# Row counts on the GpSimd queue in the last two layers of a four-layer graph network, and a few steps moved behind the output attention's preparation

## The chip, the cores and the metric

The kernel runs as one launch on one core of one Trainium2 chip. The metric is the device time of one execution in microseconds (us). A core has TensorE (PE: matmul, with weight loads shown as PEld), VectorE (DVE), ScalarE (ACT), GpSimd (POOL) and SyncE (SP). SP and POOL also issue transfers here: each has its own queue of DMA issues, taken in order.

## The reference, cut to what matters

Four graph layers over N = 4096 nodes with D = 64 features, all with the same adjacency matrix `adj` (4096 x 4096 float32, zeros and ones). Each layer is `x = x + layer(relu(layernorm(x)), adj)`.

```python
# layer 0: eight attention heads of 32 features, then an output attention
e = leaky_relu(f1[:, None] + f2[None, :], 0.2)        # per head
h = concat(elu(softmax(where(adj > 0, e, -9e15)) @ Wh) for the 8 heads)
Who = h @ W_out
e_o = leaky_relu((Who @ a1)[:, None] + (Who @ a2)[None, :], 0.2)
out0 = tanh(softmax(where(adj > 0, e_o, -9e15)) @ Who)
# layer 1: hyperbolic attention (logmap, sigmoid scores * adj, expmap), radius r, w_att, b_att
# layer 2: mean over neighbours
deg = clip(adj.sum(1) + 1, 1)
out2 = l2_normalise(relu(concat([X, (adj @ X + X) / deg]) @ W + b))
# layer 3: decaying sum over the last 100 neighbours of each row
rank = cumsum(adj != 0, axis=1); deg = rank[:, -1:]; k = minimum(deg, 100)
w = mask * where(rank - (deg - k) > 0, 0.5 ** (deg - rank), 0)
out3 = w @ (X @ weight) + bias
```

## The kernel before, in words

The nodes are held as `NB = 32` blocks of `P = 128`. Source nodes lie on the partitions, target nodes along the free axis, in groups of `G = 512` columns (`GB = 4` blocks). The kernel stores a byte mask of the edges, `mask_d`, in device memory early on; the later stages load it as tiles of `JT = 4` source blocks, so `NQ = 8` tiles make one pass over all sources.

**Counting odd entries.** The fast path assumes that `adj` holds only zeros and ones. `count_odd` (L946) proves it: it loads one block of 128 rows by `HW = 2048` columns of the float32 matrix (1 MB, tile `raw`, two buffers) and one VectorE instruction (L950) counts the entries that differ from their own `> 0`, into one column of `bad`. There are 64 such rows, taken one after the other from the iterator `todo`; every stage that has room takes some. At the end `bad` is reduced, and if anything was counted a general kernel runs instead. Before, 16 rows are counted in the output attention (every second mask tile), 11 in layer 2 and 37 in layer 3. All rows are loaded from SP's queue, the mask tiles too.

**Order.** The kernel is traced in a tile framework, and a scheduler decides at build time in what order each engine takes its instructions, buffers permitting. `behind(mark)` and `tc.issue_after(mark)` keep the instructions in their block behind a marked one, on the mark's own engine. `in_order()` keeps the traced order on PE, DVE and ACT inside its block. `staggered(...)` interleaves generators.

**Layer 0.** Each head is finished by a step (around L1711) that transposes the finished features `num` into a tile `hT` (`by_g[:, 3]`) with PE and multiplies it by `W_out`. Then comes the output attention's preparation (L1919 to L2011): a maximum over all partitions (`omax`, made by a GpSimd all-reduce, whose result L1932's neighbours wait for), the factors `YB`, `YC`, `YD1`, `YD2`, the sum over all nodes `wsum` (L1985) with its mean `meano`, and last `YCn` (L2006), whose instruction is called `prepared`. Ahead of it, in the traced order, stand the constants of layer 1 (L1746 to L1768: the radius `rt` and eleven values derived from it, loads of `wab` and `bt`) and the clearing of the tile `MOV` (L1777, 128 x 4096 bf16, on GpSimd).

The output attention has four units `u` of `HO2 = 1024` target columns. For each of the eight mask tiles `mo` (512 KB, three buffers) a unit inverts the mask into `nmo8`, stores it as `noedge_d` from POOL's queue, makes the attention's bit patterns `st` (ACT, L1200), `B` (DVE, L1206) and `C` (DVE, L1214), and lets PE accumulate `accB`, `accC` (L2097) and `dd` (L2110, L2116). `meano` is used only at the unit's end, by one product that is added to `accC`. The unit is then evicted (`evD`, `evB`, `evC`), and `finish_unit` and the node work of layer 1 run beside the next unit.

**Layer 1** works on pairs of node blocks with PE, DVE and ACT and uses the tiles `XAf`, `LDf` and `MOV`.

**Layer 2** (L2617 to L2668) has two halves of 2048 target columns: PE multiplies the mask tiles `m2` (1 MB) with the features (`nacc`, L2628) and counts degrees with a selector `sel` (`dc`, L2641). Each half is then evicted and goes through `layer2_group` four times: a serial chain of mean, concatenation `cat`, product, relu, norm, residual and layer norm, which ends with layer 3's support, in two parts `SS` and `lo` (L2609 ff.).

**Layer 3** (L2671 to L2741) has four units of 1024 columns. For each mask tile `m3` (512 KB, three buffers) and each of its four blocks `j`, PE makes the rank from the end (`pv`, L2697 and L2705), ACT turns it into the weight `w3b` (L2714), and PE accumulates `sacc` (L2679). A unit is evicted into `ev3` (L2724), folded by PE (`pn`, L2729), given bias and residual by DVE (`og`, L2737 and L2738), and stored in two pieces of 128 KB from POOL's queue (L2739). Row counts in layers 2 and 3 are held behind the last layer-norm or support instruction that is ready (`not_before_nodes`, `valued[-1]`).

Of the kernel before, what the change touches and what calls it, by code (L numbers as in the profile page):

```python
# [9 lines left out]
F32 = mybir.dt.float32  # L10
BF16 = mybir.dt.bfloat16
F16 = mybir.dt.float16
# [6 lines left out]
ALU = mybir.AluOpType  # L19
# [5 lines left out]
P = 128  # L25
N = 4096
NB = N // P
D = 64
# [10 lines left out]
PROJ_EPS = 0.004  # L39
# [12 lines left out]
HW = N // 2  # L52
# [778 lines left out]
def kernel(  # L831
# [24 lines left out]
    nc = tc.nc  # L856
    NH, F, O = W_sp.shape[0] + W_int.shape[0], W_sp.shape[1], W_sp.shape[2]
# [85 lines left out]

        return col.unsqueeze(2).to_broadcast([P, col.shape[1], width])

    def count_odd(pool, c):  # L946

        raw = pool.tile([P, HW], F32, name="raw", tag="raw", bufs=2)
        nc.sync.dma_start(raw, adjT[c % NB * P : (c % NB + 1) * P, c // NB * HW : (c // NB + 1) * HW])
        nc.vector.scalar_tensor_tensor(  # L950
            raw, raw, 0.0, raw, ALU.is_gt, ALU.not_equal, accum_out=bad[:, c : c + 1]
        )

    todo = iter(range(2 * NB))
# [81 lines left out]
    with ExitStack() as l0:  # L1036
        lp = l0.enter_context(tc.tile_pool(name="l0", bufs=1))
# [402 lines left out]
        with ExitStack() as ha:  # L1440
# [34 lines left out]
            for hf in range(2):  # L1475
# [9 lines left out]
                for hd in range(NH):  # L1485
# [61 lines left out]
                    for j0 in range(0, NB, 2):  # L1547
                        q = j0 // JT
# [111 lines left out]
                    def finish_unit(hf=hf, hd=hd, ev=ev, fme=fme):  # L1660
# [50 lines left out]
                            return  # L1711
                        c = hd // 4
                        for bq in range(NS):
                            hT = by_g[:, 3]
                            transpose_to(
                                hT, [num[:, bq * GB + b, :] for b in range(GB)], P, ps, nc.scalar.copy
                            )
                            pw = ps.tile([P, GB, D + 2], F32, name="pwho", tag="misc")
                            for b in range(GB):
                                nc.tensor.matmul(  # L1720
                                    pw[:, b, :],
                                    lhsT=hT[:, b * P : (b + 1) * P],
                                    rhs=rho[:, c, :],
                                    start=True,
                                    stop=True,
                                )
# [13 lines left out]
        lq = ctx.enter_context(tc.tile_pool(name="l1", bufs=1))  # L1740
        KA = D + 2

        def scalar_tile(name):
            return lq.tile([P, 1], F32, name=name)

        rt, rabs, sqc, cc = (scalar_tile(n) for n in ("rt", "rabs", "sqc", "cc"))  # L1746
        nc.gpsimd.dma_start(rt, r_in.unsqueeze(0).to_broadcast([P, 1]))
        nc.vector.scalar_tensor_tensor(rabs, rt, -1.0, rt, ALU.mult, ALU.max)
        nc.vector.reciprocal(sqc, rabs)
        nc.vector.tensor_tensor(cc, rt, rt, ALU.mult)  # L1750
        nc.vector.reciprocal(cc, cc)
        c2, m2c, p2c, m4c, cneg, maxn, hrow = (
            scalar_tile(n) for n in ("c2", "m2c", "p2c", "m4c", "cneg", "maxn", "hrow")
        )
        nc.vector.tensor_tensor(c2, cc, cc, ALU.mult)
        nc.vector.tensor_scalar(m2c, cc, -2.0, None, ALU.mult)
        nc.vector.tensor_scalar(m4c, cc, -4.0, None, ALU.mult)
        nc.vector.tensor_scalar(p2c, cc, 2.0, None, ALU.mult)
        nc.vector.tensor_scalar(cneg, cc, -1.0, None, ALU.mult)
        nc.vector.tensor_scalar(maxn, rabs, 1.0 - PROJ_EPS, None, ALU.mult)  # L1760
        nc.vector.tensor_scalar(hrow, rabs, 0.5, None, ALU.mult)
        wab = lq.tile([P, 2, D], F32, name="wab")
        nc.gpsimd.dma_start(
            wab.rearrange("p s d -> p (s d)"),
            w_att.rearrange("k o -> (k o)").unsqueeze(0).to_broadcast([P, 2 * D]),
        )
        bt = scalar_tile("bt")
        nc.gpsimd.dma_start(bt, b_att.unsqueeze(0).to_broadcast([P, 1]))  # L1768
# [8 lines left out]
        nc.gpsimd.memset(MOV, 0.0)  # L1777

        def layer1_nodes(bs, work, augs):

# [93 lines left out]
        with ExitStack() as ob:  # L1874
# [47 lines left out]
            with in_order():  # L1922
# [58 lines left out]
                )  # L1981
                nc.scalar.activation(wno, wno, AF.Exp, scale=1.0 - ALPHA)

                wsum = spool.tile([P, D], F32, name="wsum")
                nc.vector.tensor_reduce(wsum, vals.rearrange("p b d -> p d b"), AX.X, ALU.add)  # L1985
                pss = ps.tile([P, D], F32, name="psso", tag="misc")
# [18 lines left out]
            YCn = hp.tile([P, NB // 8, 2, 2 * D], F16, name="YCn")  # L2005
            prepared = nc.vector.tensor_scalar(  # L2006
                YCn,
                YC.rearrange("p (n i) s d -> p n i (s d)", i=2)[:, 1::4],
                -1.0,
                None,  # L2010
                ALU.mult,  # L2011
            )

            def finish_unit(u, evs):

# [44 lines left out]
            for u in range(4):  # L2060
# [6 lines left out]

                dd = ps_acc.tile([P, G], F32, name="ddo", tag="acc")
                for q in range(NQ):
                    if q % 2 == 0:  # L2070
                        with behind(prepared.ins):
                            count_odd(work, next(todo))
                    m = work.tile([P, JT, HO2], U8, name="mo", tag="mo", bufs=3)
# [48 lines left out]
                    if q == 0 and pending:  # L2122
                        finish_unit(*pending)
                        beside = layer1_nodes(slice((u - 1) * OB, u * OB), work, augs)
                        pending = None
                    elif u:
                        for _ in range(2):
                            next(beside, None)
# [332 lines left out]
    def layers_fast(es, wide, *sums):  # L2461
# [23 lines left out]
        nc.gpsimd.dma_start(w3, W3)  # L2485
        b3t = lp.tile([P, D], F32, name="b3f")
        nc.gpsimd.dma_start(b3t, b3.unsqueeze(0).to_broadcast([P, D]))
        sel = lp.tile([P, NB * O], BF16, name="sel")
        nc.gpsimd.memset(sel, 0.0)
        nc.gpsimd.memset(sel[:, :: O + 1], 1.0)  # L2490

# [76 lines left out]
        def layer2_group(b0, part, deg):  # L2568
# [6 lines left out]
                    pn[:, b, :], lhsT=part[:, b * P : (b + 1) * P], rhs=fold_h, start=True, stop=True  # L2575
                )
            cat = work.tile([P, GB, 2 * D], F32, name="cat", tag="cat")
            nc.gpsimd.tensor_copy(cat[:, :, 0:D], hg)
            nc.vector.scalar_tensor_tensor(cat[:, :, D:], pn, 1.0 / VALH, hg, ALU.mult, ALU.add)
            nc.vector.tensor_tensor(cat[:, :, D:], cat[:, :, D:], over(deg, D), ALU.mult)  # L2580
            cT = work.tile([P, G], F32, name="cT", tag="cT")
# [35 lines left out]
        with tc.tile_pool(name="ps_nacc", bufs=6, space=PSUM) as ps_acc:  # L2617
            for hf in range(2):
                accs = [ps_acc.tile([P, G], F32, name="nacc", tag="nacc") for _ in range(NS)]
                dc = ps_acc.tile([P, G], F32, name="dc", tag="nacc")  # L2620
                for q in range(NQ):
                    m = work.tile([P, JT, HW], U8, name="m2", tag="m2", bufs=3)
                    nc.sync.dma_start(m, mask_d[q][hf])
                    m8 = m.bitcast(F8)
                    for t in range(JT):
                        j = q * JT + t
                        for k in range(NS):
                            nc.tensor.matmul(  # L2628
                                accs[k],
                                lhsT=HH[:, j].rearrange("p s d -> p (s d)"),  # L2630
                                rhs=m8[:, t, k * G : (k + 1) * G],
                                start=(j == 0),
                                stop=(j == NB - 1),
                            )
# [38 lines left out]
        for u in range(4):  # L2673
# [14 lines left out]
            for q in range(NQ):  # L2688
                m = work.tile([P, JT, HO2], U8, name="m3", tag="m3", bufs=3)
                nc.sync.dma_start(m, mask_d[q][u // 2][:, :, hs])  # L2690
                for t in range(JT):
# [33 lines left out]
            for k in range(NK):  # L2725
                b0 = (u * NK + k) * GB
                pn = ps.tile([P, GB, D], F32, name="pn3", tag="misc")
                for b in range(GB):
# [10 lines left out]
                nc.gpsimd.dma_start(  # L2739
                    out[b0 * P : (b0 + GB) * P, :].rearrange("(b p) f -> p b f", p=P), og  # L2740
                )  # L2741
        assert next(todo, None) is None
# [91 lines left out]
```

## Time and profile before

| what | value |
|---|---|
| time, median of 3 runs | 2189.05 us (2187.16 to 2190.17) |
| the profiled execution's own time | 2194.35 us |
| its span, from first to last instruction | 2192.6 us |
| mean TensorE clock granted in it | 0.933 of full speed |
| PE, DVE, ACT, POOL busy | 88%, 81%, 74%, 4% of the span |

The stages lie in the trace as follows: heads of layer 0 up to 950 us, preparation of the output attention 950 to 980, its four units 957 to 1182, layer 1 to 1840, layer 2 to 1960, layer 3's units to 2013, 2066, 2138 and 2182.

How to read the lines below: a group of the profile gives the source line, engine, operation, `out<-in`, shape and count, then the total busy time in us and the mean of one in ns, then the idle time of that engine just before these instructions with what ended most of it. A window gives its length, then for each engine the busy time in us and the number of instructions, the granted TensorE clock, the busy share of the DMA engines and the rate. A timeline gives the start in us, the length, the engine or queue, the line and the instruction; on a queue such as SPq the length is how long the issue waited. A share over the whole span is a mean over stages with different limits, so the stage's own window counts.

### The profile page before, as it was taken

Reading aid. Unit: us, or ns where it says so; the run is one execution under the profiler, and the core shown is the slowest. Engines: PE = TensorE matmul, PEld = TensorE weight load, DVE = VectorE, ACT = ScalarE, POOL = GpSimd, SP = SyncE. Lnnn points to the kernel's source line nnn. Section 1 sums busy time; section 2 is a strip of 40 time slices with the busy share of each in tenths; the row PEclk is TensorE's granted clock in tenths of the full one; section 3 lists DMA queues with packets and bytes.
Section 4 is the critical chain, followed back from the end, with each engine's and each line's share of the span. In section 5 each row is a group of like instructions: output and inputs, shape, how many; then the busy total and the mean of one; then the engine's idle time right before and its main releaser. Section 6 shows DMA issues by size and latency. Waiting matters only on the chain.

```text
span 2192.6 us, 43992 instructions
## 1 busy us (share of the span) xinstructions
PE 1923.9 (88%) x19276; PEld 865.5 (39%) x19276; DVE 1765.8 (81%) x2330; ACT 1623.2 (74%) x1402; POOL 84.7 (4%) x124
## 2 busy tenths in 40 slices
PE   4989989999999999949997699999999968989878
PEld 3444444444444444423443233333333323444222
DVE  6689989997898899978986799998989987634554
ACT  4678878997798799847885778888888862146546
POOL 1000100000000000011110000000000000000000
PEclk8999999999999999959998799999999988879979
DMA  9945554343111111049751111011011133824885
GB/s 112 187 95 93 98 87 113 126 180 130 45 45 45 45 50 50 2 158 333 249 174 68 35 29 29 25 34 39 25 29 34 34 110 133 307 65 139 304 301 200
DMA packets 117008, 239.01 MB, mean 109 GB/s; under 512 B 11059, under 2 KB 84003, under 8 KB 102051
## 3 DMA queue, kind: packets, MB, share of 16 engines
q1 hardware_dynamic: 101990, 192.92, 25.6%
q0 software_dynamic: 14816, 43.18, 11.0%
q8 instruction: 153, 2.51, 0.5%
q14 instruction: 49, 0.40, 0.1%
HBM read 245.34 MB, written 49.46 MB: 134 GB/s over the span
## 4 chain that ended last, share of the span: by engine, by line
PE 30%; DVE 14%; issue 12%; ACT 6%; DMA 2%; POOL 0%; POOLq 0%; SPq 0%; DVEq 0%; ACTq 0%
PE accj L2292 6%; PE pu L2259 3%; PE acco L2097 3%; PE pl L2228 2%; PE pf L2330 2%; PE pl L2231 2%; DVE at L2281 2%; PE accC L1536 2%; DMA mo<-edges 2%; PE nacc L2628 1%; ACT sg L2215 1%; PE accB L1536 1%; ACT xt L2215 1%; DVE at L2286 1%; ACT root L2215 1%
## 5 line engine op out<-in xcount | busy, mean ns | idle before, releaser
L1200 ACT ACTIVATE st<-srow,nt 128x2048 int8<-128x2048 f32 x352 | 682.8, 1994 | 77.1 <-DVE B L1206 76.3
L1206 DVE TENSOR_TENSOR B<-st,mres 128x1024 int32<-128x1024 int32 x256 | 311.9, 1221 | 65.8 <-PE accC L1536 41.3
L1536 PE MATMUL accB<-B,ybh 128*32 128x512 fp8e4 x3072 | 338.3, 384 | 15.6 <-DVE B L1206 15.6
L1536 PE MATMUL accD<-B,ybh 128*32 128x512 fp8e4 x2048 | 300.7, 386 | 22.2 <-DVE h L1652 22.2
L1536 PEld LDWEIGHTS <-ybh 128*32 128x32 bf16 (+1 forms) x6656 | 197.1, 98 | 237.4 <-issue 75.6
L1536 PE MATMUL accC<-B,ycn 128*32 128x512 fp8e4 x2272 | 266.8, 379 | 1.2 <-issue 1.2
L1536 PE MATMUL accC<-mres,ych 128*32 128x512 fp8e4 x2272 | 266.9, 380 | 0.0
L1536 PE MATMUL accL<-B,ybh 128*32 128x512 fp8e4 x1536 | 220.2, 391 | 4.7 <-DVE h L1656 4.5
L2292 PE MATMUL accj<-sg,who 128*64 128x512 f32 (+1 forms) x512 | 199.6, 619 | 17.8 <-DVE sg L2333 6.9
L1536 PEld LDWEIGHTS <-ych 128*32 128x32 f16 x4096 | 168.4, 98 | 114.5 <-issue 9.0
L1194 DVE TENSOR_SCALAR st<-srow,nt 128x2048 uint8<-128x2048 f32 x160 | 205.5, 1285 | 2.5
L950 DVE SCALAR_TENSOR_TENSOR raw<-raw 128x2048 f32<-128x2048 f32 x64 | 146.2, 2287 | 70.4 <-DMA raw<-in_adj_dram 70.2
L2215 ACT ACTIVATE sg<-pl,rb 128x512 f32<-128x512 f32 x256 | 163.3, 684 | 48.3 <-PE pl L2231 44.0
L2292 PE MATMUL acci<-sg,who 128*64 128x512 f32 (+1 forms) x512 | 199.1, 618 | 0.0
L2714 ACT ACTIVATE w3b<-pv 128x1024 int16<-128x1024 f32 x128 | 130.0, 1023 | 82.9 <-PE pv L2705 81.8
L1200 ACT ACTIVATE st<-srowo,nto 128x1024 int8<-128x1024 f32 x128 | 137.9, 1138 | 25.4 <-DVE B L1206 25.4
L2259 PE MATMUL pu<-XAf,LDf 66*128 66x512 f32 x288 | 146.8, 612 | 7.1 <-DVE at L2266 4.7
L1536 PE MATMUL accC<-C,ych 128*32 128x512 fp8e4 x1824 | 145.7, 388 | 1.2 <-DVE C L1214 1.2
L1214 DVE TENSOR_TENSOR C<-B,mres 128x1024 int32<-128x1024 int32 x114 | 139.6, 1225 | 3.6
L1536 PEld LDWEIGHTS <-ycn 128*32 128x32 f16 x2272 | 107.4, 97 | 63.7 <-issue 2.9
L2266 DVE TENSOR_SCALAR at<-pu 128x512 f32<-128x512 f32 x144 | 95.3, 684 | 20.0 <-PE pu L2259 19.2
L2228 PE MATMUL pl<-nm,noid 128*128 128x512 fp8e4 x256 | 99.8, 390 | 10.5 <-ACT sg L2215 8.9
(497 smaller groups left out, 3132.2 us busy)
## 6 DMA issues: line engine op xcount, KB each, us to landing
raw<-in_adj_dram SPq DMA_DIRECT2D x64, 1024.0 KB, 6.6
mo<-edges SPq DMA_DIRECT2D x32, 512.0 KB, 4.3
noedge<-nmo POOLq DMA_DIRECT2D x32, 512.0 KB, 4.2
nm<-noedge SPq DMA_DIRECT2D x64, 256.0 KB, 3.0
m<-edges SPq DMA_DIRECT2D x16, 1024.0 KB, 4.8
m<-edges SPq DMA_DIRECT2D x32, 512.0 KB, 6.2
srow<-srow_d SPq DMA_DIRECT2D x15, 1024.0 KB, 6.8
mres<-in_adj_dram POOLq DMA_DIRECT2D x8, 1024.0 KB, 35.9
```

Source lines behind the costliest of these rows:

```text
L950: nc.vector.scalar_tensor_tensor(raw, raw, 0.0, raw, ALU.is_gt, ALU.not_equal, accum_out=bad[:, c : c + 1])
L1194: nc.vector.tensor_scalar(st[:, i, :].bitcast(U8), srow, negs[:, i : i + 1], EDGE, ALU.is_gt, ALU.mult)
L1200: nc.scalar.activation(st[:, i, :], srow, AF.Sign, bias=negs[:, i : i + 1], scale=-1.0)
L1206: nc.vector.tensor_tensor(B.bitcast(I32), st.bitcast(I32), edges.bitcast(I32), ALU.bitwise_and)
L1214: nc.vector.tensor_tensor(C.bitcast(I32), B.bitcast(I32), edges.bitcast(I32), ALU.bitwise_xor)
L1536: ins = nc.tensor.matmul(acc[k * O : (k + 1) * O, :], lhsT=values, rhs=moving(k), start=start, stop=stop,)
L2215: tc.keep_in_program_order(nc.scalar.activation(*args, **kw))
L2228: nc.tensor.matmul(pl, lhsT=noid, rhs=nm[:, b, :].bitcast(F8), start=True, stop=False)
L2259: nc.tensor.matmul(pu, lhsT=LD[:, j * P : (j + 1) * P], rhs=XA[:, grp(gi)], start=True, stop=True,)
L2266: nc.vector.tensor_scalar(at[:, b, :], pu, UMIN, None, ALU.max)
L2292: nc.tensor.matmul(acc[r : r + n, :], lhsT=XQ[:, src, cols], rhs=w, start=start, stop=stop)
L2714: nc.scalar.activation(w, pv, AF.Relu)
```

## The change

Seven edits:

1. Row counts of layers 2 and 3 load their rows from POOL's queue instead of SP's.
2. The split of the 64 rows is 12, 11 and 41 instead of 16, 11 and 37. In the output attention they stand at mask tiles 0, 3 and 5 of each unit; in layer 3 at fourteen blocks of unit 0 and nine of each later unit.
3. The constants of layer 1 and the clearing of `MOV` are written behind `prepared`.
4. The node sum, its mean and the spread test become a function `means`, called in unit 0 at mask tile 3, behind `prepared`.
5. `hT` takes a buffer of its own for each of the four groups of a finished head.
6. `sel` lies in the tail of `LDf`, which layer 1 has used before, instead of a tile of its own.
7. Two copies of layer 2 (`cat`, `cnt16`) go from GpSimd to ACT, and the stores of the output from POOL's queue to SP's.

```diff
-    def count_odd(pool, c):
+    def count_odd(pool, c, queue=nc.sync):
...
-        nc.sync.dma_start(raw, adjT[c % NB * P : (c % NB + 1) * P, c // NB * HW : (c // NB + 1) * HW])
+        queue.dma_start(raw, adjT[c % NB * P : (c % NB + 1) * P, c // NB * HW : (c // NB + 1) * HW])
...
-                            hT = by_g[:, 3]
+                            hT = by_g[:, bq]
...
-        rt, rabs, sqc, cc = (scalar_tile(n) for n in ("rt", "rabs", "sqc", "cc"))
-        nc.gpsimd.dma_start(rt, r_in.unsqueeze(0).to_broadcast([P, 1]))
...
-        nc.gpsimd.memset(MOV, 0.0)
...
+            YCn = hp.tile([P, NB // 8, 2, 2 * D], F16, name="YCn")
+            prepared = nc.vector.tensor_scalar(
...
+            with behind(prepared.ins):
...
+                rt, rabs, sqc, cc = (scalar_tile(n) for n in ("rt", "rabs", "sqc", "cc"))
+                nc.gpsimd.dma_start(rt, r_in.unsqueeze(0).to_broadcast([P, 1]))
...
+                nc.gpsimd.memset(MOV, 0.0)
+
+            def means():
+
                 wsum = spool.tile([P, D], F32, name="wsum")
                 nc.vector.tensor_reduce(wsum, vals.rearrange("p b d -> p d b"), AX.X, ALU.add)
...
-                    if q % 2 == 0:
+                    if q in (0, 3, 5):
                         with behind(prepared.ins):
                             count_odd(work, next(todo))
...
                         pending = None
+                    elif (u, q) == (0, 3):
...
-        sel = lp.tile([P, NB * O], BF16, name="sel")
+        sel = LD_all.bitcast(BF16)[:, NB * P : NB * (P + O)]
...
-            nc.gpsimd.tensor_copy(cat[:, :, 0:D], hg)
+            nc.scalar.copy(cat[:, :, 0:D], hg)
...
-                            count_odd(work, next(todo))
+                            count_odd(work, next(todo), nc.gpsimd)
...
-                nc.gpsimd.tensor_copy(cnt16[:, hf], cf)
+                nc.scalar.copy(cnt16[:, hf], cf)
...
-                    if (j % 4 == 1 or j == 31 and u == 1) if u else j % 5 and j > NB // 2:
+                    if (j % 4 == 1 or j == 31) if u else j > NB // 2 + 1:
                         with tc.issue_after(valued[-1].ins):
-                            count_odd(work, next(todo))
+                            count_odd(work, next(todo), nc.gpsimd)
...
-                nc.gpsimd.dma_start(
+                nc.sync.dma_start(
                     out[b0 * P : (b0 + GB) * P, :].rearrange("(b p) f -> p b f", p=P), og
                 )
```

More of the change, by code (lines that the diff above doesn't have):

```diff
@@ L1741 @@
         KA = D + 2
-        def scalar_tile(name):
-            return lq.tile([P, 1], F32, name=name)
-        rt, rabs, sqc, cc = (scalar_tile(n) for n in ("rt", "rabs", "sqc", "cc"))
-        nc.gpsimd.dma_start(rt, r_in.unsqueeze(0).to_broadcast([P, 1]))
[L1748 to L1762, printed above, removed]
-        nc.gpsimd.dma_start(
[L1764 to L1768, printed above, removed]
         a, pc, pm, pinv, pabs, left, nrb = (
@@ L1982, with scalar_tile @@
                 nc.scalar.activation(wno, wno, AF.Exp, scale=1.0 - ALPHA)
+            YCn = hp.tile([P, NB // 8, 2, 2 * D], F16, name="YCn")
+            prepared = nc.vector.tensor_scalar(
+                YCn,
+                YC.rearrange("p (n i) s d -> p n i (s d)", i=2)[:, 1::4],
+                -1.0,
+                None,
+                ALU.mult,
+            )
+            with behind(prepared.ins):
+                def scalar_tile(name):
+                    return lq.tile([P, 1], F32, name=name)
+                rt, rabs, sqc, cc = (scalar_tile(n) for n in ("rt", "rabs", "sqc", "cc"))
+                nc.gpsimd.dma_start(rt, r_in.unsqueeze(0).to_broadcast([P, 1]))
+                nc.vector.scalar_tensor_tensor(rabs, rt, -1.0, rt, ALU.mult, ALU.max)
+                nc.vector.reciprocal(sqc, rabs)
+                nc.vector.tensor_tensor(cc, rt, rt, ALU.mult)
+                nc.vector.reciprocal(cc, cc)
+                c2, m2c, p2c, m4c, cneg, maxn, hrow = (
+                    scalar_tile(n) for n in ("c2", "m2c", "p2c", "m4c", "cneg", "maxn", "hrow")
+                )
+                nc.vector.tensor_tensor(c2, cc, cc, ALU.mult)
+                nc.vector.tensor_scalar(m2c, cc, -2.0, None, ALU.mult)
+                nc.vector.tensor_scalar(m4c, cc, -4.0, None, ALU.mult)
+                nc.vector.tensor_scalar(p2c, cc, 2.0, None, ALU.mult)
+                nc.vector.tensor_scalar(cneg, cc, -1.0, None, ALU.mult)
+                nc.vector.tensor_scalar(maxn, rabs, 1.0 - PROJ_EPS, None, ALU.mult)
+                nc.vector.tensor_scalar(hrow, rabs, 0.5, None, ALU.mult)
+                wab = lq.tile([P, 2, D], F32, name="wab")
+                nc.gpsimd.dma_start(
+                    wab.rearrange("p s d -> p (s d)"),
+                    w_att.rearrange("k o -> (k o)").unsqueeze(0).to_broadcast([P, 2 * D]),
+                )
+                bt = scalar_tile("bt")
+                nc.gpsimd.dma_start(bt, b_att.unsqueeze(0).to_broadcast([P, 1]))
+                nc.gpsimd.memset(MOV, 0.0)
+            def means():
                 wsum = spool.tile([P, D], F32, name="wsum")
@@ L2002 @@
                 nc.vector.tensor_scalar(bad[:, 2 * NB + 1 :], sp, SPREAD, None, ALU.is_gt)
[L2005 to L2012, printed above, removed]
             def finish_unit(u, evs):
@@ L2125 @@
                         pending = None
+                    elif (u, q) == (0, 3):
+                        with behind(prepared.ins):
+                            means()
                     elif u:
@@ L2738, in layers_fast @@
                 nc.vector.tensor_tensor(og, og, x[:, b0 : b0 + GB, :], ALU.add)
-                nc.gpsimd.dma_start(
+                nc.sync.dma_start(
                     out[b0 * P : (b0 + GB) * P, :].rearrange("(b p) f -> p b f", p=P), og
```

## The prediction

> **What bounds the kernel now.** I read the page first (engine totals, costliest groups, DMA issues), then windows over the stretches that the change touches, then the timelines of single queues there.
>
> ```profile
> PE 1923.9 (88%) x19276; PEld 865.5 (39%) x19276; DVE 1765.8 (81%) x2330; ACT 1623.2 (74%) x1402; POOL 84.7 (4%) x124
> ...
> L950 DVE SCALAR_TENSOR_TENSOR raw<-raw 128x2048 f32<-128x2048 f32 x64 | 146.2, 2287 | 70.4 <-DMA raw<-in_adj_dram 70.2
> ...
> raw<-in_adj_dram SPq DMA_DIRECT2D x64, 1024.0 KB, 6.6
> ```
>
> PE leads and POOL is nearly idle, but these are averages. Each of the 64 counted rows costs a 1 MB transfer and 2.29 us of DVE, and DVE stood 70.2 us waiting for rows. The windows show where: the four units of the output attention, then layer 2's groups, then layer 3's units 0 to 3.
>
> ```profile
> core 0: us, PE busy (x) PEld busy (x) DVE busy (x) ACT busy (x) POOL busy (x), PEclk, DMA share, GB/s
> 957.00:1032.00 75.00, 52.55 (x304) 19.65 (x308) 69.00 (x124) 56.33 (x66) 6.87 (x10) 0.83 0.77 283
> 1032.00:1086.00 54.00, 49.52 (x354) 23.72 (x347) 47.53 (x107) 40.42 (x44) 5.71 (x8) 1.00 0.75 249
> 1086.00:1139.00 53.00, 48.01 (x320) 21.75 (x318) 46.01 (x97) 43.68 (x48) 6.42 (x9) 0.94 0.58 196
> 1139.00:1182.00 43.00, 41.97 (x297) 19.66 (x296) 29.78 (x71) 32.12 (x42) 3.56 (x5) 1.00 0.35 121
> ```
> ```profile
> 1866.00:1941.00 75.00, 60.69 (x388) 34.07 (x386) 44.35 (x88) 16.45 (x39) 3.55 (x5) 0.85 0.65 244
> 1941.00:2013.00 72.00, 69.88 (x337) 31.91 (x337) 27.09 (x70) 47.30 (x71) 0.81 (x2) 0.88 0.21 63
> 2013.00:2066.00 53.00, 47.07 (x205) 15.15 (x204) 27.71 (x29) 32.02 (x32) 1.57 (x2) 0.93 0.84 296
> 2066.00:2138.00 72.00, 56.58 (x212) 16.92 (x210) 38.73 (x38) 32.54 (x34) 1.50 (x2) 0.81 0.89 307
> 2138.00:2182.00 44.00, 42.96 (x204) 14.35 (x202) 20.82 (x24) 33.28 (x34) 1.86 (x3) 1.00 0.66 239
> ```
>
> In the output attention, unit 3, which counts no row, takes 43 us with PE full; units 1 and 2 take 54 and 53 with DVE at 87%. In layer 3 PE needs 43 us a unit (last line), yet units 1 and 2 take 53 and 72 with DMA at 0.84 and 0.89: rows set the pace.
>
> ```profile
> 2072.81 4.17 SPq L949 DMA_DIRECT2D raw<-in_adj_dram  x2
> 2077.07 0.52 SPq L2690 DMA_DIRECT2D m<-edges  x1
> 2081.24 5.26 SPq L949 DMA_DIRECT2D raw<-in_adj_dram  x2
> ```
>
> SP issues two rows, then one mask tile, which PE uses up in four column blocks of 1.31 us. A row is issued 0.1 us after a count frees one of its two buffers and lands some 7.1 us later; so a row takes (7.1 + 2.3 + 0.1)/2 = 4.7 us at most, and the 16 counts that start from 2066.4 to 2133.4 show 4.46. The mask comes every 9 us, and PE waits with it.
>
> **What the Trainium skill says.** "Trainium Kernel Development and Optimization", Key Constraints: transfers issued from SP, ACT and POOL run on the same 16 DMA engines, and another issuer saves only issue time. So POOL's queue adds no bandwidth. "DMA: Bandwidth & Descriptors", Latency and other measured facts: the first byte takes about 1 us from POOL and 0.6 us from SP. The trace can't show it: 512 KB land in 4.2 us from POOL (a store) and 4.3 from SP (a load). "SBUF — State Buffer", Who interferes with whom: DVE in a two-port mode and GpSimd exclude each other for a whole instruction. The trace agrees:
>
> ```profile
> 953.36 3.54 POOL L1777 MEMSET MOV<- 128x4096 bf16 x1
> ...
> 954.51 2.41 DVE L1932 TENSOR_SCALAR mx<-mx 128x2 f32<-128x2 f32 x1
> ...
> 976.18 3.98 DVE L1985 TENSOR_REDUCE wsum<-who 128x64 f32<-128x2048 f32 x1
> ```
>
> Its neighbour on 128x4 takes 0.17 us; it ended when the clearing did. POOL's issues of transfers took 0.71 to 0.75 us all through the count's stages, so I let counts not hold them up.
>
> **The change part by part.**
>
> *Clearing and constants.* The helper orders only what runs on the marked instruction's engine, DVE. In the built order of the changed kernel POOL still clears MOV before the all-reduce `omax`: the 2.2 us lost at L1932 stay. The 11 constants (some 0.08 us each) ran while DVE waited for that all-reduce; behind the preparation they cost 0.8 us of a busy DVE. Sum +0.8, from 0 to +1.
>
> *Node sum.* L1985's 3.98 us stand ahead of YCn (L2006), for which PE waits 3.6 us. They leave that place and come back inside unit 0, where DVE is 92% busy. I take -1; from -4 (absorbed) to +2 (order).
>
> *Four counts fewer in the output attention* (7, 3, 2, 0 a unit by the built order, against about 9, 4, 3, 0). DVE is relieved of 4 x 2.29 = 9.2 us, DMA of 4 MB. PE idles 10 (from 970), 4.5, 5 and 1 us in the units, 20 in all: the ceiling. DVE was 87 to 92% busy, so I take nine tenths of 9.2, -8; from -3 to -15.
>
> *hT in four buffers.* In the last unit each copy to hT waited for PE's transposes, not for the products that read hT, and PE's built order is still transposes, products, transposes. Nothing; from -1 to 0.
>
> *Layer 2.* The same 11 rows, but in the built order on DVE nine of them stand within its first two groups, and none in the third and fourth (before: 4, 2, 2, 1 after the first two). A group's chain is serial, 14.8 us without rows (1964.5, 1979.3, 1993.7 for the starts of L2579). As a row lands only every 4.5 us, the eleventh can't start before 1870.4 + 8 x 4.5 = 1906.4; without waiting the chain would be there at 1903. So +3; from -2 (SP's mask tiles are no longer behind rows) to +9 (4.8 us a row, and PE's stream out of step).
>
> *Copies to ACT.* Eight of 0.42 us and two of 0.59 (rows of those shapes); ACT is busy 16 of 75 and 47 of 72 us there. Covered: 0; up to +2 if one falls into a chain. `sel` cleared in LD's tail: POOL 1.3 us, after layer 1's last use, unwatched: 0. If LD were read later than I think, the first `dc` products would wait, +1.
>
> *Layer 3's rows on POOL's queue.* After unit 0, the changed order on DVE has 35 counts up to unit 3's eviction, as before, but then 4 more, three of them behind the last outputs. From unit 0's eviction (2012.9) to the end it was 179.7 us. Now: 35c + 4 x 4.2 (rows without masks) + 7 (after the last count: 5.0 to SP's last wait, as from 2175.0 to 2180.0, and 2.0 to close). For c: POOL reacts 0.3 us after DVE (L2079) against 0.1, first byte +0.4 by the skill, so +0.6 a cycle or +0.3 a row; against that DMA was idle 11 to 16%, and neither queue now stops behind the other. I take 4.45: 155.8 + 16.8 + 7 = 179.6, no change. Ends: c = (4.8 the fastest landing + 2.3 + 0.4)/2 = 3.75, 155 us, -25; c = 5.0, 199 us, +19. What is late next: the counts themselves, since SP's masks are free. Stores on SP stand after three masks of the next unit, which its three buffers take at once: 0; the last store lands before the last count.
>
> **Sum**: +0.8 - 1 - 8 + 3 + 0, about -6. The profiled execution took 2194.35 us around its span of 2192.6, 5.3 above the median; taken off the median of 2189.05 it is 2183.
>
> **Rivals.** *(1) Slower: the row's cycle grows on POOL's queue.* Place: DVE's order in layer 3, where eviction and output stand behind the counts. At c = 4.9 it costs 35 x 0.45 = 16 us, and with layer 2 at +6 and the output attention at -7 that is +15: 2204. It decides from c = 4.62. For it: the buffer cycle already binds, and the skill's first byte. Against: 512 KB land alike from both queues. *(2) Much faster: the single FIFO was the brake.* Two rings fill the idle 13% of DMA: c = 4.0 gives 140 + 16.8 + 7 = 164, -16, in all some -22: 2167. For it: 0.93 to 1.03 of DMA and 331 to 389 GB/s from 990 to 1030 us, with both queues at work. Against: POOL's two tiles in flight are the same two. *(3) No change:* only the four moved counts do anything, and their 8 us come back as four rows of 4.2 in the tail; two of the named parts (clearing, hT) do nothing anyway.
>
> **Numbers.** A measurement of this kernel tells 0.2%, 4.4 us, from no change. Main case 0.36, rival (2) 0.15, so faster 0.51; rival (3) 0.18; rival (1) 0.31. The range goes from rival (2)'s lower part, 2161, to rival (1)'s 2206.
>
> **What would show it.** Right: L1932 still 2.4 us; wsum inside unit 0 and YCn 2 to 4 us earlier; units 1 and 2 of the output attention near 50 us; layer 2's last `lo` some 3 us later; layer 3's units 1 to 3 even, some 52 to 55 us; four counts after PE's last product. Wrong: row counts under 4.2 or over 4.7 us apart in layer 3; POOL issues well over 0.75 us; PE waiting for masks again.

## The result and the profile after

The changed kernel takes 2212.72 us in the median of 4 runs (2209.88 to 2217.87), the one before 2188.11 in the same comparison; the ratio is 1.0118, 95% interval 1.0093 to 1.0143. In a later comparison on another chip (run e8) it was 1.0098, 1.0073 to 1.0124. The span of the profiled execution grew from 2192.6 to 2209.8 us, by 17.2; a single profiled execution may lie up to 7 us off the median of its kernel (in e2, 2198.00 against 2204.79).

The page's group of the counts and its transfers come first (columns as before: busy time and mean, then idle time and what ended it; then KB each and median us to landing).

```profile
L950 DVE SCALAR_TENSOR_TENSOR raw<-raw 128x2048 f32<-128x2048 f32 x64 | 146.4, 2289 | 92.9 <-DMA raw<-in_adj_dram 92.9
...
raw<-in_adj_dram POOLq DMA_DIRECT2D x52, 1024.0 KB, 6.7
...
m<-edges SPq DMA_DIRECT2D x16, 1024.0 KB, 6.4
m<-edges SPq DMA_DIRECT2D x32, 512.0 KB, 4.9
...
raw<-in_adj_dram SPq DMA_DIRECT2D x12, 1024.0 KB, 6.6
```

VectorE now stands 92.9 us before rows that have not landed, against 70.2. In the median a row lands as fast as ever, 6.7 us against 6.6. The medians of the masks moved, layer 2's 1 MB tiles from 4.8 to 6.4 us and layer 3's 512 KB tiles from 6.2 to 4.9, but the same kernel in e8 has 4.8 and 6.0 again, so nothing can be read from them.

The windows of the changed kernel follow: the four units of the output attention, the first half of layer 2, then layer 3's units 1 to 3 and the tail behind the last eviction.

```profile
957.00:1024.00 67.00, 47.25 (x286) 18.17 (x287) 61.27 (x116) 50.71 (x61) 7.05 (x11) 0.85 0.79 280
1024.00:1072.00 48.00, 45.18 (x307) 20.30 (x307) 43.02 (x96) 38.36 (x43) 4.99 (x7) 0.96 0.72 246
1072.00:1117.00 45.00, 44.75 (x314) 20.61 (x313) 41.91 (x93) 40.00 (x45) 5.69 (x8) 1.00 0.58 193
1117.00:1163.00 46.00, 45.32 (x320) 21.30 (x318) 36.32 (x86) 36.39 (x41) 4.98 (x7) 1.00 0.43 150
1856.00:1931.00 75.00, 57.38 (x364) 30.95 (x361) 39.29 (x73) 14.12 (x35) 4.88 (x10) 0.83 0.64 247
```
```profile
2018.00:2071.00 53.00, 44.96 (x216) 15.62 (x214) 26.75 (x26) 33.24 (x33) 5.80 (x11) 0.95 0.90 318
2071.00:2127.00 56.00, 48.77 (x208) 16.12 (x208) 29.82 (x30) 33.24 (x33) 6.33 (x12) 0.87 0.86 300
2127.00:2182.00 55.00, 45.78 (x202) 15.58 (x202) 29.16 (x30) 32.30 (x32) 6.33 (x12) 0.90 0.82 287
2182.00:2209.00 27.00, 1.97 (x8) 1.78 (x8) 11.96 (x17) 0.00 (x0) 1.95 (x4) 0.50 0.41 131
```

The output attention's units 1 and 2 are now as short as unit 3, with PE full. Layer 3's units 1 to 3 are even and all three bound by rows (transfer engines at 0.82 to 0.90, PE at 45 to 49 of 53 to 56 us), and 27 us follow in which PE does 2 us of work.

To compare kernels I cut each span at landmarks of VectorE's timeline: the last `evD` (end of the output attention), the first and second instruction of a group's `cat` (start of layer 2's first group), the fourth and eighth `lo`, and the first `ev3` (unit 0's eviction). All columns are differences of such starts, in us. "Row" is the time from unit 0's eviction to the end of the last count, divided by the counts in it (39 or 35).

| kernel | output attention ends | layer 1 | layer 2, first half | second half | layer 3 from unit 0's eviction to the end | row | span | ratio of the runs to before |
|---|---|---|---|---|---|---|---|---|
| before | 1174.6 | 693.7 | 72.5 | 67.4 | 179.7 | 4.63 | 2192.6 | 1 |
| after | 1162.3 | 696.2 | 87.6 | 66.9 | 192.1 | 4.64 | 2209.8 | 1.0118 |
| e1, rows on SP again | 1164.0 | 697.1 | 72.4 | 67.5 | 187.8 | 4.51 | 2193.6 | 0.9992 (0.9981 to 1.0004) |
| e2, split back | 1172.3 | 693.3 | 87.6 | 66.9 | 171.2 | 4.56 | 2196.0 | 1.0051 (1.0039 to 1.0064) |
| e3, only the rest | 1169.2 | 693.0 | 72.4 | 67.6 | 177.0 | 4.56 | 2183.8 | 0.9987 (0.9978 to 0.9997) |
| e4, only the queue | 1174.2 | 696.1 | 83.8 | 66.9 | 179.6 | 4.72 | 2205.3 | 1.0093 (1.0074 to 1.0111) |
| e5, counts spread | 1162.0 | 696.2 | 75.7 | 67.6 | 194.0 | 4.69 | 2200.2 | 1.0051 (1.0036 to 1.0065) |
| e6, layer 2 on SP | 1166.0 | 697.6 | 72.3 | 67.5 | 196.5 | 4.71 | 2204.7 | 1.0048 (1.0029 to 1.0067) |
| e8, changed again | 1164.9 | 697.5 | 83.9 | 66.9 | 189.8 | 4.57 | 2207.7 | 1.0098 (1.0073 to 1.0124) |

So between the two profiled executions: output attention -12.3, layer 1 +2.5, layer 2's first half +15.1, its second half -0.5, layer 3 +12.4; in sum 17.2.

### The profile page after: what moved, and what is told of

The parts are those of the page before. It is cut to its first block, busy times and chain, and to the rows that moved or that the text cites. A ratio compares the mean times of both kernels' runs of the same rounds, so it can differ in the third digit from the quotient of the medians.

```text
span 2209.8 us, 43972 instructions
## 1 busy us (share of the span) xinstructions
PE 1918.5 (87%) x19276; PEld 868.8 (39%) x19276; DVE 1765.5 (80%) x2330; ACT 1626.5 (74%) x1412; POOL 100.3 (5%) x158
## 4 chain that ended last, share of the span: by engine, by line
PE 24%; issue 21%; DVE 10%; ACT 5%; POOL 2%; DMA 2%; POOLq 0%; SPq 0%; DVEq 0%
PE accj L2298 6%; PE pu L2265 3%; PE pl L2234 2%; PE pf L2336 2%; PE acco L2100 2%; PE pl L2237 2%; DVE at L2287 2%; PE accC L1536 2%; ACT sg L2221 1%; PE accB L1536 1%; ACT st L1200 1%; POOL raw L949 1%; DVE at L2292 1%; DVE B L1206 1%; ACT xt L2221 1%
## 5 line engine op out<-in xcount | busy, mean ns | idle before, releaser
L1536 PEld LDWEIGHTS <-ybh 128*32 128x32 bf16 (+1 forms) x6656 | 197.1, 98 | 237.5 <-issue 75.7
L950 DVE SCALAR_TENSOR_TENSOR raw<-raw 128x2048 f32<-128x2048 f32 x64 | 146.4, 2289 | 92.9 <-DMA raw<-in_adj_dram 92.9
L2720 ACT ACTIVATE w3b<-pv 128x1024 int16<-128x1024 f32 x128 | 130.9, 1023 | 67.6 <-PE pv L2711 66.2
```

The lines of the kernel that those rows point to most:

```text
L950: nc.vector.scalar_tensor_tensor(raw, raw, 0.0, raw, ALU.is_gt, ALU.not_equal, accum_out=bad[:, c : c + 1])
L1536: ins = nc.tensor.matmul(acc[k * O : (k + 1) * O, :], lhsT=values, rhs=moving(k), start=start, stop=stop,)
```

## The experiments

### Queue and split, each undone (e1 to e4)

e1 takes the changed kernel and loads the rows of layers 2 and 3 from SP again:

```diff
-                            count_odd(work, next(todo), nc.gpsimd)
+                            count_odd(work, next(todo))
```

> The changed kernel with the rows of layers 2 and 3 loaded from SP's queue again; the 12/11/41 split and all else as changed. Theory A (the loss is made of two parts: in layer 2 the GpSimd queue makes the scheduler put nine counts into the first two groups, +15 us; in layer 3 the four extra rows stand behind the last outputs, +16 us; the output attention gives back 12): the built order of layer 2 is that of before again, so the first to the second group's support take the time of before, the tail of layer 3 stays, and the kernel comes to 2213 - 15 = 2198 us. Rival B (a row takes longer on GpSimd's queue everywhere, layer 3 included): layer 3 from unit 0's eviction to the end falls from 192 to about 182 us as well, and the kernel is near 2188. Rival C (the queue does nothing): stays at 2213.

Measured: 0.9992 of before. Layer 2's first half is 72.4 us again, to 0.1 us of before. Layer 3 takes 187.8 us, between theory A (192) and rival B (182). So the queue carries nearly the whole loss; theory A had its first half right and put too little on layer 3, where the queue costs another 4 us in this pair of profiles.

e2 shares the rows out 16/11/37 again and keeps the queue:

```diff
-                    if q in (0, 3, 5):
+                    if q % 2 == 0:
...
-                    if (j % 4 == 1 or j == 31) if u else j > NB // 2 + 1:
+                    if (j % 4 == 1 or j == 31 and u == 1) if u else j % 5 and j > NB // 2:
```

> The changed kernel with the rows shared out 16/11/37 again; queues and all else as changed. Theory A: four more counts in the output attention cost 8 to 10 us there, the tail behind the last outputs loses four rows of 4.4 us (some 16), so the kernel falls by 6 to 8, to about 2206 us; layer 2 stays 15 us too long. Rival B (rows slow on GpSimd's queue): about the same here, but the counts of layer 3 are still over 4.6 us apart and the end still lies on them. Rival C (the output attention's gain comes from the moved preparation, not from fewer counts): the gain there stays and the kernel falls by the full 16, to 2197.

Measured: 1.0051, some 10 us below the changed kernel's 1.0098 in e8 (15 below its first 1.0118). The output attention ends 10.0 us later than in the changed kernel (1172.3) and layer 3 is 20.9 us shorter: the tail behind the last outputs is gone. With the rows on GpSimd's queue four of them are thus worth about 2.5 us each in the output attention and 5 in layer 3, where nothing covers them. Rival C falls: most of the gain in the output attention went with the rows.

e3 undoes both and keeps the rest (moved preparation, `hT`, `sel`, copies on ACT, stores on SP).

> Queue of the rows and split as before; what stays of the change is the moved clearing, constants and node sum, four buffers for hT, sel in LDf's tail, copies to ACT, stores from SP. Theory A: these are worth -1 to -4 us in all (the node sum alone), so 2185 to 2188. Rival C (the preparation carries the gain of the output attention): -8 to -12 us, 2176 to 2180. Rival D (the copies to ACT or the stores on SP lengthen layers 2 and 3): slower than before by 3 us or more.

Measured: 0.9987 (0.9978 to 0.9997), some 3 us faster, as theory A had it. The rest as a whole does no harm; its parts were not run one by one.

e4 is the kernel before with the queue alone:

```diff
-        nc.sync.dma_start(raw, adjT[c % NB * P : (c % NB + 1) * P, c // NB * HW : (c // NB + 1) * HW])
+        queue.dma_start(raw, adjT[c % NB * P : (c % NB + 1) * P, c // NB * HW : (c // NB + 1) * HW])
```

> The kernel before with one thing changed: rows of layers 2 and 3 from GpSimd's queue. Theory A: layer 2 has the changed kernel's order on VectorE (nine counts in the first two groups) and loses some 15 us; layer 3 has 37 rows at about the same 4.6 us and the order 2, 12, 12, 11 between evictions, so its end comes at most 3 us later than 15: 2202 to 2207 us. Rival B (rows slow on GpSimd's queue): layer 3 from unit 0's eviction to the end goes from 180 us to over 186, and the kernel to 2210 or more. Rival E (layer 2's loss comes from the copies moved to ACT, not from the queue): no change, 2189.

Measured: 1.0093, 20 us by the ratio, 12.7 by the span. Layer 2's first half is 83.8 us, so the copies on ACT (rival E) have nothing to do with it. Layer 3 takes 179.6, as before. By spans this is theory A; by the runs it lies nearer to rival B.

With "the rest" in place, four kernels form a square. With all rows on SP's queue the old split gives 0.9987 (e3) and the new one 0.9992 (e1): by the runs the split costs nothing there, though the two profiled executions lie 9.8 us apart. With GpSimd's queue it is 1.0051 (e2) and 1.0098 or 1.0118 (changed). VectorE's order shows why. Between the evictions of layer 3 and behind the last one, e1 has 13, 17, 9 and 0 counts, the changed kernel 11, 12, 12 and 4. So the tail behind the last outputs is there only together with GpSimd's queue.

### Why layer 2 is longer: order or transfers (e5, e6)

The timeline of VectorE in the changed kernel shows the first group of layer 2 (start, length, then in brackets the idle time before and its releaser):

```profile
1867.25 2.29 DVE L950 SCALAR_TENSOR_TENSOR raw<-raw 128x2048 f32<-128x2048 f32 x1 [3.58 <-DMA raw<-in_adj_dram]
1869.47 0.08 DVE L950 DVE_READ_ACCUMULATOR raw<-raw 128x1 f32 x1
1869.47 0.42 DVE L2600 TENSOR_REDUCE nrm<-sq 128x4 f32<-128x256 f32 x1
...
1873.00 2.29 DVE L950 SCALAR_TENSOR_TENSOR raw<-raw 128x2048 f32<-128x2048 f32 x1 [0.89 <-DMA raw<-in_adj_dram]
1875.22 0.08 DVE L950 DVE_READ_ACCUMULATOR raw<-raw 128x1 f32 x1
1875.22 0.42 DVE L968 TENSOR_TENSOR h<-x,ln_mean 128x256 f32<-128x256 f32 x1
...
1878.27 2.29 DVE L950 SCALAR_TENSOR_TENSOR raw<-raw 128x2048 f32<-128x2048 f32 x1 [1.73 <-DMA raw<-in_adj_dram]
1880.48 0.08 DVE L950 DVE_READ_ACCUMULATOR raw<-raw 128x1 f32 x1
1880.48 0.17 DVE L980 RECIPROCAL ln_var<-ln_var 128x4 f32<-128x4 f32 x1
```

A count stands in VectorE's order before a step of the group (`nrm`, `h`, `ln_var`). Its row is not there, and the step, though its own inputs may be, waits for the row and then for the 2.29 us of counting. Over layer 2's first half VectorE waited for rows as follows (us in total, times), first in the changed kernel (1840 to 1935 us), then before (1850 to 1945):

```profile
  DMA raw<-in_adj_dram: 12.2, 7
```
```profile
  DMA raw<-in_adj_dram: 1.1, 1
```

PE feels it: its wait for `h` (line 981, ahead of the transposes) went from 11.5 to 22.6 us over the four groups. e5 keeps GpSimd's queue and only spreads the counts:

```diff
-                        with not_before_nodes():
+                        with tc.issue_after(valued[q // 2 - 1].ins) if hf and q > 1 else not_before_nodes():
                             count_odd(work, next(todo), nc.gpsimd)
```

> The changed kernel, rows still on GpSimd's queue, but the second half's rows of layer 2 are held behind the support of the first, second and third group (two each), so that VectorE's order has 2 to 3 counts a group as before. From the first group's start to the fourth support it was 72.5 us before and 87.6 in the changed kernel. Theory A1 (VectorE stands in its order before a count whose row has not landed, and the group's chain behind it): 73 to 77 us, and the kernel falls by 10 to 15 us. Rival A2 (on a queue of their own the rows compete with SP's 1 MB mask tiles, so rows and masks land late whatever the order): over 82 us, the kernel falls by less than 5.

Measured: the first half takes 75.7 us, and the kernel falls from 1.0098 to 1.0051, some 10 us. VectorE's wait for rows there is down to

```profile
  DMA raw<-in_adj_dram: 5.3, 3
```

A1 holds for most of it: on the same queue another place of the counts takes back 8 to 12 of the 11 to 15 us, so A2 can't be the whole cause. What e5 leaves lies in the first group: from its first `cat` to its `lo` it takes 23.4 us, against 27.2 in the changed kernel and 17.4 before. There the rows share full transfer engines with the masks in the changed kernel (shown under layer 2 below); that this is what e5 leaves is likely, not shown. The crowded order with the rows on SP's queue was not run.

> The changed kernel with only layer 2's rows on SP's queue; layer 3's stay on GpSimd's. Theory A: layer 2's first half takes 72.5 us again, layer 3 stays as in the changed kernel (192 us from unit 0's eviction to the end), so it falls by 15 us. Rival B (layer 3's queue costs more than that): it falls no further than the changed kernel with both on SP is, which lies 4 us lower in layer 3 (188).

e6 brings layer 2 back to 72.3 us and the kernel to 1.0048, about 11 us below the changed one. But e1, with layer 3 on SP too, is at 0.9992: by the runs layer 3's queue costs another 12 us at 41 rows (by the spans 8.7: 196.5 against 187.8). In the four profiles with 41 rows on GpSimd's queue (after, e5, e6, e8) a row takes 4.57 to 4.71 us, on SP's 4.51. That is theory A plus a part of rival B. With 37 rows the queue shows no such cost: e2 and e3 both have 4.56 us a row. The order of the counts differs in each of these pairs as well, so a cost of the queue itself in layer 3 is not shown.

> The changed kernel once more, on the same chip as the three above and in more rounds. By the stages of the profiles it lies 17 us above the one before (output attention -12, layer 1 +2.5, layer 2 +15, layer 3 +12), by the runs on record 25. If the stages hold, the ratio is 1.008 to 1.010; if there is a part that they do not show, 1.011 to 1.013.

e8 gave 1.0098, within what the stages show. Its interval reaches up to 1.0124, so a part of a few us that the stages do not show is not excluded.

### Where the rows would go (e7, e9, e10, e11)

Layer 3 is bound by rows, while layer 2's second half has the transfer engines at 0.2 and VectorE at a third. e7 sets the fourteen rows of unit 0 free there:

```diff
-                        with tc.issue_after(valued[-1].ins):
+                        with tc.issue_after(valued[-1 if u else NS - 1 + (j - NB // 2 - 1) // 4].ins):
```

> The changed kernel with all rows on SP's queue and the fourteen rows of layer 3's unit 0 set free earlier: held behind the supports of layer 2's fourth to seventh group (3, 4, 4 and 3 of them) instead of the eighth. There DMA is at 0.2 and VectorE at 23 of 72 us, while PE is full. If layer 3 is bound by rows (4.45 us each, 41 of them in 188 us against 3 x 43.5 us of PE), then fourteen fewer there leave 27 rows x 4.45 = 120 us, PE becomes the bound, and layer 3 from unit 0's eviction to the end takes 142 to 150 us, the kernel 2148 to 2158. If instead the counts delay the serial chain of layer 2's second half (67 us) and PE behind it, up to 15 us come back: 2165 or more.

Measured: 0.9901 (0.9875 to 0.9926), 2171.56 us. Layer 3 falls to 146.5 us, as computed for PE as the bound, but layer 2's second half grows from 67.5 to 89.9. Both halves of the expectation came true. In the waits of that stretch PE stands before the transposes for what VectorE's chain delivers late (us in total, times, longest; PEld's wait is 1.2 us in e9 below):

```profile
PEld tr L995 <- DVE h L981: 18.0, 4, 9.3
PE tr L995 <- DVE h L981: 16.2, 3, 8.8
```

e9 therefore puts one count behind each group's `cat` and one behind its finished layer norm, where VectorE waits for PE anyway, eight in all:

```diff
+            gaps.append(
+                nc.vector.tensor_tensor(cat[:, :, D:], cat[:, :, D:], over(deg, D), ALU.mult).ins
+            )
...
+            gaps.append(nc.cur_bb.bb.instructions[-1])
...
+                        held = valued[-1].ins
+                        if u == 0 and early:
+                            held = gaps[early.pop(0)]
+                        with tc.issue_after(held):
+                            count_odd(work, next(todo))
```

> The changed kernel with all rows on SP's queue; eight of the fourteen rows of layer 3's unit 0 are set free in layer 2's second half, one behind each group's concatenation and one behind each group's finished layer norm, where VectorE waits 4 to 5 us for PE in any case; the other six stay behind the eighth support. If a count is free where VectorE waits for PE: layer 2's second half stays at 67 to 71 us (it was 90 with thirteen rows bunched there), layer 3 has 33 rows x 4.45 = 147 plus the close, some 155 to 160 us, and the kernel is near 2160 (the bunched one: 2171). If rows cost the chain their 2.3 us wherever they stand, the half takes 67 + 8 x 2.3 = 85 us and the kernel 2175.

Measured: 0.9867 (0.9851 to 0.9883). The second half takes 67.5 us with eight rows in it: they cost nothing. Layer 3 takes 163.0, a little more than the 155 to 160 expected. e10 gives layer 2's own eight rows of the second half the same treatment.

> As the run with rows in the gaps, and layer 2's own eight rows of its second half placed the same way in the first half's groups, one a gap. Theory A1 (place decides): the first half falls from 72 us to 62 to 68, 15.5 us a group as in a group without rows, and the kernel by 4 to 8 us against that run. Rival (the first half is bound by PE's product stream or by the rate of rows, 4.5 us each): stays at 72.

Measured: 0.9837 (0.9823 to 0.9852), 2156.68 us, the fastest of all and some 36 us below the kernel before in the same comparison. Layer 2's first half falls from 72.3 to 60.3 us. The timeline of its third group shows the form to aim at:

```profile
1891.12 0.42 DVE L2587 TENSOR_TENSOR cat<-cat,degf 128x256 f32<-128x256 f32 x1
1891.46 2.28 DVE L950 SCALAR_TENSOR_TENSOR raw<-raw 128x2048 f32<-128x2048 f32 x1
1893.67 0.08 DVE L950 DVE_READ_ACCUMULATOR raw<-raw 128x1 f32 x1
1894.17 0.42 DVE L2597 TENSOR_TENSOR zt<-pz,b2f 128x256 f32<-128x256 f32 x1 [0.42 <-PE pz L2593]
```

The count starts without a wait, because its row landed long ago, and ends 0.42 us before PE delivers `pz`. Layer 3 now has units 2 and 3 at PE's pace:

```profile
1994.00:2052.00 58.00, 50.51 (x216) 16.98 (x220) 33.67 (x32) 32.27 (x33) 0.00 (x0) 0.90 0.89 307
2052.00:2096.00 44.00, 42.38 (x196) 13.55 (x196) 23.27 (x25) 32.91 (x33) 0.00 (x0) 1.00 0.92 322
2096.00:2140.00 44.00, 42.57 (x201) 14.45 (x204) 23.11 (x25) 33.28 (x34) 0.37 (x1) 1.00 0.78 282
```

> As the run with both kinds of rows in gaps, but layer 3's 41 rows from GpSimd's queue. With masks and rows on two queues, and 33 rows left between unit 0 and the end. Theory A (the queue itself is neutral or costs up to 0.2 us a row: 4.57 to 4.65 us on GpSimd's, 4.45 on SP's): 0 to 7 us slower than the same on SP's. If two queues fill the transfer engines better when the rows are not the bound, units come nearer to PE's 43.5 us and it is faster by 5 us or more.

e11 is at 0.9866 (0.9851 to 0.9882), 6 us above e10, with layer 3 at 167.5 us against 156.6. Of these 10.9 us some 6 lie in the 32 rows (4.69 us each against 4.50) and 4.6 behind the last count. That is slower too, at the far end of what was expected for a neutral queue; VectorE's order in layer 3 changed as well (12, 12, 8 counts a unit against 14, 9, 9).

### The stores (e12)

> The kernel before with the rows on GpSimd's queue and the output's stores on SP's: only these two edits. With the queue alone layer 3 took 179.6 us from unit 0's eviction to the end, with queue and all else but the split 171.2. If a store that waits for its output on GpSimd's queue holds back the row issues behind it, this kernel has 170 to 173 us there and is 6 to 9 us faster than the queue alone (1.009 of before): 1.005 to 1.006. If the difference was chance or another edit, it stays at 1.009.

e12 is inconclusive. Its layer 3 takes 173.3 us, near the 170 to 173 of the expectation and 6.3 below the queue alone, but the ratio is 1.0087 (1.0066 to 1.0107), no different from e4's 1.0093. So layer 3 fits the theory of a store that holds back row issues, but the time doesn't show it, and it stays open.

## Why the prediction was wrong, point by point

**Clearing and constants: right.** GpSimd still clears `MOV` ahead of the all-reduce, and line 1904 (1932 before) still waits for it:

```profile
953.67 3.54 POOL L1993 MEMSET MOV<- 128x4096 bf16 x1
...
954.83 2.40 DVE L1904 TENSOR_SCALAR mx<-mx 128x2 f32<-128x2 f32 x1
```

**Node sum and four counts fewer: right in the sum.** It was to be +0.8 - 1 - 8 us; the output attention came out 12.3 us shorter, inside the ranges given. `wsum` starts at 990.0, inside unit 0, and `YCn` 1.3 us earlier (978.78), less than the 2 to 4 named. Over all profiles the output attention ends at 1174.2 to 1176.6 us with the old preparation (before, e4, e12), at 1169.2 to 1172.3 with the moved parts and 16 rows (e2, e3), and at 1162.0 to 1166.0 with 12 rows. In the mean the moved parts are worth 4 us, where the text had 0.2, and the rows 7, where it had 8.

**Layer 2: the step that failed first.** The text gave +3 us, at most +9; measured +15.1 (+11.4 in e8). All of it lies in the first two groups, which take 53.4 us from the first `cat` to the second `lo`, against 37.5 before. The text had read nine counts there, but took late rows as one delay, at the eleventh ("the eleventh can't start before 1906.4"). Its two times belong to before's clock, yet moved to the earlier start of layer 2 they still give some +3, so the clock is not the error. The third count started at 1860.82 and the eleventh at 1903.58, so a row took 42.76/8 = 5.3 us instead of 4.5. And the delay was no single one: VectorE stood before rows at seven counts, 12.2 us in all, and each of these counts stands before another step of the serial chain. The group had come 9.8 us earlier (its first `cat` at 1858.47 against 1868.28); the whole lead was waited away and 5.3 us more.

One end of the range rested on an effect that came out the other way. "SP's mask tiles are no longer behind rows" was counted as up to -2. In the changed kernel SP issued four mask tiles from 1853.3 to 1867.5 us with no row between them, while the group's first rows were on their way, and the transfer engines were full:

```profile
1856.00:1874.00 18.00, 17.94 (x130) 8.99 (x127) 10.91 (x22) 3.00 (x7) 1.19 (x3) 1.00 1.01 421
```

A row issued at 1855.61 in this stretch landed 11.6 us later; before, no row of layer 2's first half took more than 7.6. e5 and e6 take back 8 to 15 us, e5 with the place of the counts alone. e10 shows the same eleven rows at no visible cost in other places: its first two groups, with five counts in them, take 29.5 us, the 14.8 a group that the text has for a group without rows.

**Layer 3: a term that was mis-sized.** The text had 179.6 us and no change; measured 192.1, against 179.7 before. The rate c = 4.45 us was the interval inside a unit. By the measure in which it was used, from unit 0's eviction to the end of the last count, the kernel before took 2175.0 - 2012.9 = 162.1 us for 35 rows, 4.63 each: the turns between units belong to it. In the same place of the sum the changed kernel took 164.8 us where the text had 155.8 (+9.0, of which 6.3 were there before the change). The four rows of the tail took 16.1 us where it had 16.8. The close was 11.3 us, not 7 (+4.3). Units 1 to 3 came even, as forecast (53.7, 55.7 and 55.4 us), and four counts stand behind the last eviction. The tail on the timeline:

```profile
2182.45 0.69 DVE L2730 COPY ev<-sacc 128x512 f32<-128x512 f32 x1
2183.06 2.28 DVE L950 SCALAR_TENSOR_TENSOR raw<-raw 128x2048 f32<-128x2048 f32 x1
...
2188.23 2.29 DVE L950 SCALAR_TENSOR_TENSOR raw<-raw 128x2048 f32<-128x2048 f32 x1 [1.55 <-DMA raw<-in_adj_dram]
2190.45 0.08 DVE L950 DVE_READ_ACCUMULATOR raw<-raw 128x1 f32 x1
2190.82 0.53 POOL L949 DMA_DIRECT2D raw<-in_adj_dram  x1 [4.65 <-DVE raw L950]
2191.44 2.29 DVE L950 SCALAR_TENSOR_TENSOR raw<-raw 128x2048 f32<-128x2048 f32 x1 [0.92 <-DMA raw<-in_adj_dram]
...
2196.24 2.29 DVE L950 SCALAR_TENSOR_TENSOR raw<-raw 128x2048 f32<-128x2048 f32 x1 [2.50 <-DMA raw<-in_adj_dram]
```

**The sum.** The terms of the text give -5.2, which it rounded to -6. The profiles show +17.2: 12.1 more than forecast in layer 2's first half, 12.4 more in layer 3, 2.5 in layer 1, and 4.1 less in the output attention (0.5 less in layer 2's second half).

**The rivals.** Rival (1) named the right place and side, and its threshold of 4.62 us was passed; but most of its excess over 4.45 was there before. What came with the queue is between nothing (e2 against e3) and 0.2 us a row (e6 against e1); with 41 rows 2 to 9 us in layer 3. Rival (2) falls: two queues moved no more bytes, 287 to 318 GB/s in layer 3's units against 239 to 307 before with the same row rate. That agrees with what the Trainium skill states in "Trainium Kernel Development and Optimization", Key Constraints: another issuer saves only issue time. Rival (3) had the tail's price right, and the output attention's gain was indeed given back there; layer 2 came on top.

**hT, copies, `sel`: nothing speaks against the text.** e3, the whole rest together, is some 3 us faster than before; the single parts were not told apart.

**What stays open.** Layer 1 grew by 2.5 us. Over all profiles it lies between 693.0 and 698.8 us, and why is not shown. Why a row of layer 3 is slower from GpSimd's queue in most profiles with 41 rows (the reaction of 0.3 us instead of 0.1, the competition with masks that run ahead, or VectorE's other order) wasn't told apart.

## What to carry to other kernels

A background task on an in-order engine costs what stands behind it: place each piece in a gap where that engine waits for another, with its data already there, and here it cost nothing (e9, e10). Bunched into a serial chain, nine pieces in two groups cost 11 to 15 us more than the six of before did, and thirteen in layer 2's second half cost 22 (e7). When a transfer moves to another queue, read the new built order of the engine that consumes it, because the scheduler may move the consumer too: the queue alone turned 4, 2, 2, 1 counts in layer 2's groups into 5, 4, 0, 0 (e4). Take a rate from the stretch in which it will be used, turns between units included, and not from the best part of it.

## What was not expected of the hardware

A row issue took GpSimd 0.53 us, where its stores had taken 0.71 to 0.75. Masks and rows on two queues shared the engines differently, not better. Beside rows, and as far as the trace has their landing, layer 2's 1 MB mask tiles landed 8.9 to 9.6 us after their issue in one queue, and 6.4 to 7.5 in two (4.7 to 7.3 in e8). The slowest row of that stretch went the other way, from 7.6 to 11.6 us (9.7 in e8).
